# A two-layer kernel on one core: where the shared expert's last products, sums and first additions stand between layer 0 and layer 1

## The chip, the core and the metric

The kernel runs on one NeuronCore of a Trainium2 chip. The time is the device time of one execution in microseconds (us). The profile comes from one further execution that the hardware profiler recorded. The engines are named as in the profile: PE is TensorE's matmul, PEld its weight load, DVE is VectorE, ACT is ScalarE, POOL is GpSimd, SP is SyncE, which here only issues transfers. A name such as L908 is a line of the kernel before.

## What is computed

Two transformer layers over 2048 tokens of 128 channels, all in float32. Both begin with a normalisation and an attention. Layer 0 goes on with a mixture of 16 experts of which each token uses one, plus a shared expert that every token passes. Layer 1 goes on with a gated channel mix. Cut to the part around the change:

```python
h = layernorm(x) * (1 + cb) + sb                      # layer 0, second half
logits = h @ router_w.T
top_vals, top_idx = top_k(logits, 1)                  # one expert of 16 for each token
routed = sigmoid(top_vals) * h                        # sent to that expert alone
expert_sum = (up * silu(gate)) @ down_proj            # gate, up = routed @ gate_up_proj
shared = silu(h @ shared_gate_w.T) * (h @ shared_up_w.T) @ shared_down_w.T
x = x + gb * (shared + expert_sum)
h = layernorm(x) * (1 + ca) + sa                      # layer 1, first half
k, v, q = h @ Wk, h @ Wv, h @ Wq                      # causal attention follows
```

## The kernel before

The tokens lie in 16 tiles of 128, and four tiles make a block of 512 (`TB` = 4, `NB` = 4). `x` stays in SBUF as tiles of 128 tokens by 128 channels; each half of a layer adds its result to it.

**Layer 0's end.** The attention runs over blocks and groups of heads. While its last block is being attended, blocks 0 to 2 are already normalised and routed. What is left when the attention's last weights are done is written out by hand as a list of small steps in `last0`, and `tc.manual_schedule` makes PE, DVE and ACT carry them out in just this order. The list does two things side by side. It finishes block 3: `divide`, `turn_back`, `project`, then the normalisation (`moment`, `norm`, `turn`), the router (`choose`), each token's place in its expert's list (`place`), and `send`, whose four indirect DMAs from POOL (L799) write the rows to DRAM by expert. Between these steps it computes the shared expert for block 0 in four quarters `k`: `up(k, 0)` and `up(k, 1)` are the gate's and the up projection's matmuls (L888), `silu(k)` is ACT's activation (L893), `times(k)` is DVE's product (L897), and `down(k)` adds the quarter's down projection to a sum in PSUM (L901). Quarters 0 and 1 use two PSUM tiles, and quarters 2 and 3 use them again. `add` puts the sum into `x` (L908).

One step of the list is `tiles` (L846 to L870), a chain of small DVE operations. From the count of tokens of each expert it works out how many tiles of 128 each expert needs, and leaves in `nth_i` the start row and the expert of each of the 31 tiles. SP loads the start rows into registers (L1008) and then reads each tile from DRAM (`xs`, L1018). PE loads the expert numbers into registers in the same way, later.

**The experts.** After layer 0 the shared expert has twelve quarters left, four for each of the blocks 1 to 3. `shared_step` takes one: two halves of matmuls (`shared_up`, L991), then the down projection of the quarter before (`shared_down`, L979), then ACT's Silu (L965) and DVE's product (L971; both in `shared_act`). At a block's last quarter `shared_down` also adds the block's sum to `x` (L984). Three quarters run while the tiles are fetched. Then `xs` is transposed by PE (L1031), the experts run over quads of four tiles, and three more quarters are strewn among them. The experts' results go to DRAM (`y_rows`, L1063). Sixteen indirect DMAs on POOL gather them by token (`yx`, L1096) while PE works on the last six quarters.

**Layer 1's beginning**, still in the written order. After the last Silu, ACT changes its table to Sqrt (`table`, L1160). `add(0)` adds the gathered rows of block 0 to `x` (L1110); `moments` takes mean and variance (L204, L205), the root (L217) and its reciprocal (L219); `norm` makes the normalised rows (L252), and `turn` transposes them on PE (L259) and lets ACT write `h2` (L260). The same follows for block 1. `keys` and `queries` are matmuls (L295) whose results ACT scales into a temporary (L296) and DVE writes (L297); `values` is L1127. Then ACT changes to the Exp table, the written order ends, and layer 1's attention starts (L411 is its first scores).

The list at the end of layer 0 closes so:

```python
lambda: up(2, 0), lambda: silu(2), lambda: send(made[0]), lambda: ends_at(made[1]),
lambda: up(2, 1), lambda: up(3, 0), lambda: silu(3), lambda: up(3, 1), tiles,
lambda: times(2), lambda: down(2), lambda: times(3), lambda: down(3), add]
```

## Time and profile before

| | us |
|---|---|
| median of 3 runs (lowest to highest) | 1252.55 (1251.54 to 1255.32) |
| the profiled execution's own time | 1254.59 |
| its span, from the first to the last instruction | 1252.9 |
| PE busy in it | 1156.8 (92%) |
| DVE busy | 943.9 (75%) |
| ACT busy | 780.3 (62%) |
| POOL busy | 94.4 (8%) |

The mean clock granted to TensorE is 0.944 of full speed. Start times are counted from the span's start. In the timelines a line gives the start, the duration, the engine, the line of the kernel, the operation, what it writes and reads, how many such instructions follow each other, and in brackets how long the engine was idle before it and what ended that. In the table of stretches a line gives the stretch, its length, the busy time of PE, PEld, DVE, ACT and POOL with their instructions in brackets, the granted clock, the DMA engines' share and GB/s. The chain of waits is the chain of work that ended last, followed back from the last instruction.

### The profile page before, as it was taken

What the parts mean: (1) busy time and instruction counts of PE and PEld (TensorE: products, weight loads), DVE (VectorE), ACT (ScalarE), POOL (GpSimd) and SP (SyncE); (2) the same over time, 40 slices, a digit from 0 to 9 for tenths busy, and PEclk for the clock granted to TensorE, in tenths of its full rate; (3) what the DMA queues carried; (4) which work ended last, traced back from release to release, by engine and by line L of the source; (5) the groups of instructions that cost most, each with busy time, mean ns of one, the idle gap of its engine ahead of it and who ended that gap; (6) DMA issues with size and microseconds to landing.
All of it is one profiled execution on the core that took longest, in us unless ns stands there. A gap on an engine that the chain in (4) does not pass through costs nothing.

```text
span 1252.9 us, 22356 instructions
## 1 busy us (share of the span) xinstructions
PE 1156.8 (92%) x9230; PEld 523.6 (42%) x9230; DVE 943.9 (75%) x1462; ACT 780.3 (62%) x853; POOL 94.4 (8%) x157
## 2 busy tenths in 40 slices
PE   4579999999999999999999999979978989999985
PEld 2233434444343443443344333447734444444432
DVE  3888898889889889889889983343378788897134
ACT  6107777777777777777777778743333455656763
POOL 2002000000000000000000000320232011110113
PEclk9658999999999999999999999999977899999987
DMA  4841010203220213110000000032210101000001
GB/s 122 112 52 35 2 52 1 70 27 77 69 69 12 59 36 98 38 52 2 1 3 2 1 2 2 20 122 76 66 45 7 35 1 35 1 1 2 2 1 34
DMA packets 63094, 45.22 MB, mean 36 GB/s; under 512 B 6608, under 2 KB 56912, under 8 KB 62480
## 3 DMA queue, kind: packets, MB, share of 16 engines
q1 hardware_dynamic: 60224, 40.37, 13.2%
q0 software_dynamic: 1024, 2.10, 0.6%
q10 hardware_dynamic: 1744, 1.32, 0.6%
q8 instruction: 73, 1.20, 0.4%
q14 instruction: 29, 0.24, 0.1%
HBM read 9.88 MB, written 21.95 MB: 25 GB/s over the span
## 4 chain that ended last, share of the span: by engine, by line
PE 82%; DVE 10%; ACT 4%; issue 1%; DMA 1%; POOL 1%; ACTq 0%; POOLq 0%; DVEq 0%
PE a0bank L502 24%; PE a0p L476 17%; PE a0p L411 13%; PE a1bank L502 5%; PE a1p L476 4%; DVE a0mx L415 3%; DVE a1mx L415 2%; PE a1p L411 2%; PE a1p L482 2%; PE sg L991 2%; DVE a1masked L420 2%; ACT a0e L486 1%; PE gu L1043 1%; PE a0bank L533 1%; PE sum L979 1%
## 5 line engine op out<-in xcount | busy, mean ns | idle before, releaser
L415 DVE TENSOR_REDUCE a0mx<-a0p 128x2 f32<-128x1024 f32 x512 | 624.0, 1225 | 75.9 <-PE a0p L411 66.5
L486 ACT ACTIVATE a0e<-a0p 128x1024 f32<-128x1024 f32 x512 | 522.6, 1025 | 171.9 <-PE a0p L476 146.2
L502 PE MATMUL a0bank<-a0e,vA 128*32 128x256 f32 x4096 | 333.4, 392 | 0.8 <-ACT a0e L486 0.8
L411 PE MATMUL a0p<-kS,a0qS 64*128 64x512 f32 x1024 | 248.1, 480 | 24.7 <-DVE a0mx L415 13.0
L476 PE MATMUL a0p<-a0qS,kS 64*128 64x512 f32 x1024 | 260.6, 498 | 0.0
L486 ACT ACTIVATE a1e<-a1p 128x1024 f32<-128x1024 f32 (+3 forms) x160 | 143.1, 897 | 97.6 <-PE a1p L482 92.3
L476 PEld LDWEIGHTS a0p<-a0qS,kS 64*128 64x128 f32 x1024 | 97.3, 184 | 204.5 <-issue 128.7
L411 PEld LDWEIGHTS a0p<-kS,a0qS 64*128 64x128 f32 x1024 | 100.3, 192 | 109.4 <-ACT a0e L486 56.8
L502 PEld LDWEIGHTS a0bank<-a0e,vA 128*32 128x32 f32 x4096 | 86.4, 108 | 137.9 <-issue 124.4
L415 DVE TENSOR_REDUCE a1mx<-a1p 128x2 f32<-128x1024 f32 x96 | 115.8, 1222 | 17.8 <-PE a1p L411 17.2
L502 PE MATMUL a1bank<-a1e,vA 128*32 128x256 f32 (+1 forms) x1152 | 96.9, 385 | 0.4 <-POOL a1e L489 0.4
L476 PE MATMUL a1p<-a1qS,kS 64*128 64x512 f32 (+3 forms) x320 | 76.3, 463 | 4.9 <-DVE a1mx L415 3.7
L411 PE MATMUL a1p<-kS,a1qS 64*128 64x512 f32 (+3 forms) x320 | 67.7, 422 | 11.2 <-DVE a1mx L420 4.4
L420 DVE CUSTOM_DVE_ANT_0 a1masked<-a1p,later 128x128 f32<-128x128 f32 (+3 forms) x128 | 62.6, 489 | 13.4 <-PE a1p L411 7.5
L799 POOL DMA_INDIRECT sent<-hs,row_i x16 | 15.9, 995 | 712.6 <-DVE ln11xn L252 689.5
L482 PE MATMUL a1p<-a1mT,a1ones 64*128 64x512 f32 (+3 forms) x320 | 62.2, 375 | 0.0
L476 PEld LDWEIGHTS a1p<-a1qS,kS 64*128 64x128 f32 x320 | 31.5, 189 | 61.6 <-issue 32.3
L411 PEld LDWEIGHTS a1p<-kS,a1qS 64*128 64x128 f32 x320 | 32.2, 195 | 39.5 <-DVE a1mx L420 11.5
L489 POOL TENSOR_SCALAR_AFFINE_SELECT a1e<-a1e 128x256 f32<-128x256 f32 x64 | 26.0, 406 | 255.4 <-ACT a1e L486 255.4
L502 PEld LDWEIGHTS a1bank<-a1e,vA 128*32 128x32 f32 x1152 | 25.8, 109 | 42.8 <-issue 32.6
L445 ACT CAST a0mT<-a0bank 8x512 fp32r<-8x512 f32 x16 | 9.2, 576 | 45.4 <-PE a0bank L444 45.4
L482 PEld LDWEIGHTS a1p<-a1mT,a1ones 64*128 64x128 f32 x320 | 32.2, 193 | 2.3 <-issue 1.7
(340 smaller groups left out, 718.2 us busy)
## 6 DMA issues: line engine op xcount, KB each, us to landing
sent<-blank SPq DMA_DIRECT2D x68, 256.0 KB
kS<-a0qS SPq DMA_DIRECT2D x28, 128.0 KB
wgu_sb<-in_gate_up SPq DMA_DIRECT2D x1, 2048.0 KB
a0qS<-a0qh SPq DMA_DIRECT2D x62, 32.0 KB
a0qS<-a0ql SPq DMA_DIRECT2D x62, 32.0 KB
xs<-sent SPq DMA_DIRECT2D x31, 64.0 KB
y_rows<-y SPq DMA_DIRECT2D x7, 256.0 KB
a1qS<-a1qh SPq DMA_DIRECT2D x24, 64.0 KB
```

What stands on the lines that cost most here:

```text
L411: nc.tensor.matmul(ps[:, j, :n], qS[b][r:r + RT, st, i * P:(i + 1) * P], kS(st)[r:r + RT, kb * QB:kb * QB + n], start=True, stop=True)
L415: nc.vector.tensor_reduce(pm[:, i, 2 * pair:2 * pair + 2, kb], ps, AX.X, ALU.max)
L420: nc.vector.tensor_tensor_reduce(masked[:, :n], ps[:, j, :n], later[:, QB - n:], 1.0, LOWEST, ALU.add, ALU.max, pm[:, i, g, kb:kb + 1])
L476: nc.tensor.matmul(ps[:, j, q0:], kS(st)[r:r + RT, kt * P:(kt + 1) * P], qS[b][r:r + RT, st, q0:], start=True, stop=fused)
L482: nc.tensor.matmul(ps[:, j, q0:], ones[r:r + RT, g // S, :], shift[u][r:r + RT, q0:], start=False, stop=True)
L486: nc.scalar.activation(e[:, :, q0:], ps[:, :, q0:], AF.Exp, scale=scale)
L489: nc.gpsimd.affine_select(out=e[:, :, q0:q0 + P], in_=e[:, :, q0:q0 + P], compare_op=ALU.is_ge, fill=0.0, base=0, pattern=[[0, 2], [1, P]] ...
L502: nc.tensor.matmul(av[g * W:(g + 1) * W, c0:c1], vA(kt, grp * HG + g), held[kt, g // 2][:, g % 2, c0:c1], start=(kt == 0 and c0 == 0), sto ...
L533: nc.tensor.transpose(ps[:, i * P:(i + 1) * P], o[:, i * P:(i + 1) * P], ident)
L799: nc.gpsimd.indirect_dma_start(out=sent[t], in_=hs[:, i, :], in_offset=None, out_offset=bass.IndirectOffsetOnAxis(ap=row_i.bitcast(U32)[:, ...
L979: nc.tensor.matmul(sums[b][:, i * P:(i + 1) * P], act[:, i * P:(i + 1) * P], wsd[:, k, :], start=(k == 0 and i == 0), stop=(k == NS - 1), ...
L991: nc.tensor.matmul(ps[:, j, :], w[:, k * P:(k + 1) * P], hT[:, b * QB:(b + 1) * QB], start=True, stop=True)
```

## The change

At the end of layer 0 the second halves of quarters 2 and 3 come ahead of their Silu, and `tiles` takes a function `between`, which it calls twice in the middle of its chain: there `times(2)` and `down(2)`, then `times(3)` and `down(3)` are issued. They used to stand behind the whole of `tiles`.

At the beginning of layer 1 one more quarter of the shared expert leaves the loop. Its matmuls are followed at once by those of the last quarter, and two sums are issued only after them. `add(0)` becomes four additions of one tile each, and each stands before that tile's statistics. The last quarter's product (`last_times`) moves to where the root is computed, and its sum, with the addition of block 3's result, moves from between the queries to right behind `add(1)`, ahead of block 1's statistics. `statistics` takes the number of parts as an argument; with its default it issues what it did.

```diff
+    def moments(b, name, root=False, between=lambda: None, before=lambda i: None):
-        mv, steps = statistics(b, name)
-        for step in steps:
+        mv, steps = statistics(b, name, TB)
+        for i, step in enumerate(steps):
+            before(i)
             step()
...
-    def tiles():
+    def tiles(between):
...
         nc.vector.tensor_tensor(over, ntile.unsqueeze(1).to_broadcast([P, NE, NE]), earlier,
                                 ALU.mult)
+        between(2)
         nc.vector.tensor_reduce(base, over, AX.X, ALU.add)
...
         nc.vector.memset(nth, 0.0)
+        between(3)
         nc.vector.tensor_reduce(nth[:, 1, :SLOTS], passed[:, :, 1:], AX.X, ALU.add)
...
-                lambda: up(2, 0), lambda: silu(2), lambda: send(made[0]), lambda: ends_at(made[1]),
-                lambda: up(2, 1), lambda: up(3, 0), lambda: silu(3), lambda: up(3, 1), tiles,
-                lambda: times(2), lambda: down(2), lambda: times(3), lambda: down(3), add]
+                lambda: up(2, 0), lambda: up(2, 1), lambda: silu(2), lambda: send(made[0]),
+                lambda: ends_at(made[1]), lambda: up(3, 0), lambda: up(3, 1), lambda: silu(3),
+                lambda: tiles(lambda k: (times(k), down(k))), add]
...
-        def add(b):
-            ts = slice(b * TB, (b + 1) * TB)
+        def add(b, part=slice(0, TB)):
+            ts = slice(b * TB + part.start, b * TB + part.stop)
...
-        while len(shared) > 1:
+        while len(shared) > 2:
             shared_step()
+        shared_act(*shared_up())()
         up = shared_up()
-        shared_down()
         last_times = shared_act(*up)
         table(AF.Sqrt)
-        add(0)
-        normed[0] = moments(0, "ln20", True)
+        shared_down()
+        shared_down()
+        normed[0] = moments(0, "ln20", True, last_times, lambda i: add(0, slice(i, i + 1)))
         norm(0)
         turn(0, bank)
-        last_times()
         add(1)
+        shared_down()
         normed[1] = moments(1, "ln21", True, lambda: keys(0, bank)())
...
-        shared_down()
         queries(2, po.tile([P, QB], F32, name="qs2", tag="y"))
```

More of the change, by code (lines that the diff above doesn't have):

```diff
@@ L195, in two_layers, with statistics @@
     lnp = ctx.enter_context(tc.tile_pool(name="lnp", bufs=2))
-    def statistics(b, name):
+    def statistics(b, name, parts=2):
         stats = lnp.tile([P, TB, nc.vector.BN_STATS_DIM], F32, name=name + "stats", tag="stats")
@@ L205, in some @@
                 nc.vector.bn_aggr(mv[:, i, :], stats[:, i, :])
-        return mv, [lambda: some(0, TB // 2), lambda: some(TB // 2, TB)]
-    def moments(b, name, root=False, between=lambda: None):
-        mv, steps = statistics(b, name)
-        for step in steps:
+        return mv, [lambda lo=lo: some(lo, lo + TB // parts) for lo in range(0, TB, TB // parts)]
+    def moments(b, name, root=False, between=lambda: None, before=lambda i: None):
+        mv, steps = statistics(b, name, TB)
+        for i, step in enumerate(steps):
+            before(i)
             step()
```

## The prediction

> **What bounds the kernel now.** I read the page's chain of waits first: PE has 82% of it, DVE 10%. The attention lines (L502, L476, L411, L415) carry most and the change leaves them alone, so I went to the two stretches it edits: layer 0's end (815 to 860 us) and layer 1's beginning (884 to 932 us), by the timeline of each engine. Layer 0's end:

> ```profile
> 836.20 0.42 DVE L852 TENSOR_TENSOR over<-ntile,earlier 128x256 f32<-128x256 f32 x1
> ...
> 840.31 0.18 DVE L870 CAST nth_i<-nth 1x64 int32<-1x64 f32 x1
> 840.41 1.27 DVE L897 TENSOR_TENSOR s0act<-s0act,s0ps 128x512 f32<-128x512 f32 x2
> 841.14 3.78 PE L901 MATMUL s0ps<-wsd_sb,s0act 128*128 128x128 f32 x16 [2.34 <-DVE s0act L897]
> 843.15 15.87 SPq L1018 DMA_DIRECT2D xs<-sent  x31
> 844.96 0.69 DVE L908 TENSOR_TENSOR x<-x,s0ps 128x512 f32<-128x512 f32 x1 [3.28 <-PE s0ps L901]
> 845.70 2.08 PE L991 MATMUL sg<-hT,wsg_sb 128*128 128x512 f32 x2 [0.78 <-DVE x L908]
> ...
> 855.68 1.07 PE L1031 MATMUL xsT_ps<-ident,xs 128*128 128x128 f32 x8 [0.30 <-issue]
> ```

> PE finished its last `up` at 838.79 and stood 2.34 us until the tiles' numbers were done and DVE had made `times(2)`. The first L991 then waited for the `add` (L908). So PE waits for DVE twice. The granted clock comes from the stretches view, which I cut at the clock's own changes:

> ```profile
> 833.65:837.06 3.41, 2.59 (x6) 0.68 (x4) 3.16 (x10) 0.64 (x2) 1.50 (x2) 1.00 0.47 130
> 837.06:840.48 3.42, 1.12 (x2) 0.30 (x2) 3.21 (x10) 0.56 (x1) 2.57 (x3) 1.00 0.12 38
> 840.48:843.89 3.41, 2.75 (x13) 2.75 (x14) 1.20 (x3) 0.00 (x0) 0.00 (x0) 0.50 0.06 19
> 843.89:847.30 3.41, 2.63 (x7) 1.57 (x7) 0.69 (x1) 0.00 (x0) 0.00 (x0) 0.50 0.40 116
> 847.30:850.72 3.42, 3.42 (x5) 1.35 (x4) 0.45 (x1) 0.60 (x1) 0.00 (x0) 0.50 0.47 132
> ```

> Layer 1's beginning:

> ```profile
> 906.60 0.69 DVE L1110 TENSOR_TENSOR x<-x,yx 128x512 f32<-128x512 f32 x1
> ...
> 908.57 1.28 ACT L1160 ACT_TABLE_LOAD   x1
> ...
> 910.91 1.23 PE L259 MATMUL a1bank<-ident,ln20xn 128*128 128x128 f32 x4 [2.08 <-DVE ln20xn L252]
> ...
> 918.28 1.40 PE L979 MATMUL sum<-wsd_sb,acts 128*128 128x128 f32 x8
> ...
> 923.86 0.44 PE L411 MATMUL a1p<-kS,a1qS 64*128 64x128 f32 x4 [1.09 <-DVE a1qS L297]
> ```

> ACT's last Silu ends 908.57, the table load 909.85, block 0's root 910.27; PE stands 2.08 us for the normalised rows. The clock halves from 912.16 to 918.98, and PE then bounds keys, queries and sum until 922.3.

> **Part A: layer 0's end.** No instruction is added or removed, none moved issues a DMA. GpSimd's four sends (835.25 to 840.24) keep their place; only `nth_i` shifts for SP.
> - PE: `up(2,0)` starts 833.15 as now. Now `up(k,1)` waits for `silu(k)` (L888 idle 0.69 and 0.75); both gates now come first. Four halves at 0.86 (pace of L991 at full clock): 833.15 + 3.44 = 836.6, tail to 836.75.
> - `silu(2)` waits for both halves: 835.05 to 835.65. `silu(3)`: 836.8 to 837.4.
> - DVE: `times(2)` after L852: 836.66 to 837.34, so `down(2)` 837.4 to 838.5 (1.13, as the L901 at 827.48). `times(3)` after L854, L857, L861: 838.6 to 839.3; `down(3)` 839.3 to 840.4.
> - The chain of the tiles' numbers carries both: `nth_i` ends 840.49 + 1.27 = 841.76. The `add` follows (sums long ready): 841.7 to 842.37. First L991 at 842.42 instead of 845.70: **3.28 us**.
> - Clock, on the traced grid: 837.06 to 840.48 now has some 2.2 of 3.42 us busy, kept. 840.48 to 843.89 has 1.4 to 1.5, lost. 843.89 to 847.30 is full (three steps of L991 in a row), returned. One halved stretch instead of three.
> - PE until the gathered rows: six `up` halves pairs and two sums, 3 x 1.72 + 2 x 0.89 = 6.94 us at full clock. 842.42 to 843.89 does 1.47, the halved stretch 1.71, the remaining 3.76 end 851.07. PE's own load of `nth_i` (L1008, 2.32 us, from 853.3 now, just after the second step's `times`) starts about 849.1, ends 851.4: xsT at 851.4 instead of 855.68, **-4.3 us**.
> - What hides the later `nth_i`: SP's load of it (L1008, 2.16 us, straight after the cast) ends 843.95 instead of 842.7, first xs read at 844.42, one each 0.51 us. The eighth goes out at 848.0; to landing I have no row for it, the nearest (sent 2.2, yx 2.5, at most 3.1) give 850.2 to 851.1. Needed about 851.9. Cover is 0.8 us; gone, each us late is a us lost.
> - `times` beside GpSimd's sends: ln21xn beside the gathers took 436 ns against 344, so 0 to 0.2 us; I take 0.
> Bounds: the clock falls at 840.48 too or stays down, -3.3; it never falls, PE would end 849.4 and the load 849.6, -6.1 (xs would then bind). I take -4.3.

> **Part B: layer 1's beginning** (times of the trace before the shift).
> - The last two gates run together and the sums go behind: last L991 ends 907.04 instead of 907.93, Silu 907.68, table 908.97, ready 909.18.
> - DVE: the 0.69 add becomes four of 128x128 (L538: 0.29). A tile is add, L204, L205 with 0.1 us of gaps and overlap: 0.71, x4 from 906.60: 909.5 against 909.01. Root 909.55 to 909.83. `times(3,3)` runs beside it, 909.44 to 910.12; reciprocal 910.04 against 910.29. Gain 0.25.
> - The gathers reach block 0 at 903.90 and block 1 at 908.80 (landings in the trace), before use.
> - PE: four transposes, then the sum that stood at 918.28, in front of keys. It fills the wait for hT (0.87 idle now) at full clock; halved it takes 1.8, ending 913.9.
> - New wait: block 3's add (L984, 0.69) is now ahead of block 1's statistics and waits for that sum: it ends 913.64 (full) or 914.6 (half), statistics (1.70) 915.3 or 916.3 against 914.68. Behind them ACT's root and the scaled keys, so kS starts 916.3 or 917.25 against 915.84. That is a loss at this point.
> - After kS: qS0, norm(1), qS1, qS2, vA, qS3: DVE needs 4.4 to 5.0 and no longer carries L984 and `times`. Last qS ends 921.4 at full clock. Halved with the clock back near 918, PE's queries end 921.1 and the last qS 922.6. Now it ends 923.80. So -2.4 or -1.2; should PE stay halved throughout, keys to last query take it to some 925.5, minus a return that comes at latest one full stretch on: bound +0.5.
> With the shift of part A the grid cuts the 2 us gap in two (0.97 and 1.02 idle), so full clock is rather likelier: I take **-1.8**.

> Sum: -4.3 - 1.8 = -6.1. The profiled execution took 1254.59 us (span 1252.9 and 1.7 around it): 1248.5. It lies 2.0 above the median of 1252.55, and the other runs may have their grid elsewhere; the same difference on the median gives **1246.5**.

> [...]

> **Rivals.**
> 1. The clock eats it: it halves at 840.48 too and stays down at layer 1. Then only the earlier start is left: -3.3 and 0, 1249.2. For: the grid isn't tied to the program, and the gaps left (0.9 and 2.0 us) fill one stretch on many phases. Against: the traced phase. 0.20.
> 2. Neither gap halves it: -6.1 - 2.4 = -8.5, 1244.0. For: 0.59 busy kept it. Against: 2.0 us of wait for the `add` remains. 0.20.
> 3. Slower: the shift moves layer 1's opening on the clock grid. From 925 to 985 us the mean clock is 0.69, so 22.8 of 60 us are at full. If all ran halved and half of it lies on the chain, it costs 11.4: +5.3, 1257.9. It decides from 6.1 us of chain work lost to half clock. Against: from 985 on the clock is 1.00, and the same 3.41 us rule would have to fail almost every stretch. 0.05.
> 4. It doesn't do what it says: the first L991 is not set free by the `add`, or xs lands late. Part A falls to -2 to -3, total near 1248. Against: L991 starts 0.05 after L908 ends. 0.05.

> **Numbers.** Forecast 0.50, its own range 1244.5 to 1248.6. About 0.3% (3.8 us) is what a measurement can tell from no change: faster means under 1248.8. Forecast, rival 2 and part of 4 lie there: 0.72; rival 1 and the edges 0.23; slower 0.05. Range 1243.0 (rival 2 with 1 us of spread, the runs shown span 3.8) to 1250.6 (part A at -3.3 with part B at +0.5, and 0.9 of spread).

> **What would show it.** L901 in two groups of 8, among the tiles' lines; first L991 3.3 us earlier against L888; one halved stretch there, not three; xsT 4.3 us earlier; SP's first xs read some 1.3 us later; at layer 1 the L979 directly behind L259 and the last L297 1.2 to 2.4 us earlier against L1031. It is wrong if PE waits for xs, if kS is late and nothing makes it up, or if halved stretches after 925 us grow.

## The result and the profile after

| | before | after |
|---|---|---|
| median (lowest to highest), six runs each | 1253.07 us (1251.54 to 1255.32) | 1247.64 us (1246.41 to 1249.66) |
| profiled execution | 1254.59 us | 1248.58 us |
| its span | 1252.9 us | 1246.9 us |
| mean granted clock | 0.944 | 0.947 |

The ratio is 0.9956, with a 95% interval of 0.9942 to 0.997: faster by 5.4 us, and by 6.0 us between the two profiled executions. The forecast was 6.1 us and 1246.5 us. The changed kernel is three lines longer behind the change, so L888 is now L891, L901 is L904, L908 is L911, L979 is L982, L991 is L994, L1031 is L1034 and L297 is L298.

Layer 0's end in the timeline of the changed kernel, PE first, then DVE and SP:

```profile
837.67 1.16 PE L904 MATMUL s0ps<-wsd_sb,s0act 128*128 128x128 f32 x8 [0.46 <-DVE s0act L900]
839.31 1.16 PE L904 MATMUL s0ps<-wsd_sb,s0act 128*128 128x128 f32 x8 [0.49 <-DVE s0act L900]
842.38 1.10 PE L994 MATMUL sg<-hT,wsg_sb 128*128 128x512 f32 x2 [1.91 <-DVE x L911]
849.85 1.07 PE L1034 MATMUL xsT_ps<-ident,xs 128*128 128x128 f32 x8 [0.21 <-issue]
...
836.93 0.68 DVE L900 TENSOR_TENSOR s0act<-s0act,s0ps 128x512 f32<-128x512 f32 x1
838.64 0.61 DVE L900 TENSOR_TENSOR s0act<-s0act,s0ps 128x512 f32<-128x512 f32 x1
841.46 0.18 DVE L873 CAST nth_i<-nth 1x64 int32<-1x64 f32 x1
841.56 0.67 DVE L911 TENSOR_TENSOR x<-x,s0ps 128x512 f32<-128x512 f32 x1
```

The sum that was one block of sixteen matmuls and 3.78 us at half clock is now two groups of eight among the tiles' numbers, 1.16 us each. PE's wait is at the `add`: 1.91 us. The first shared matmul behind it starts at 842.38; the forecast said 842.42. The transposes of the fetched rows start at 849.85 where 851.4 was forecast and 855.68 stood before. The clock says why, in the stretches of the changed kernel on the clock's grid (length, then busy time of PE, PEld, DVE, ACT and POOL, then clock, DMA share and GB/s):

```profile
840.90:844.31 3.41, 1.93 (x5) 1.00 (x6) 1.26 (x4) 0.00 (x0) 0.00 (x0) 1.00 0.06 19
844.31:847.72 3.41, 3.41 (x15) 1.81 (x14) 1.38 (x2) 1.20 (x2) 0.00 (x0) 1.00 0.33 96
```

No stretch is at half clock; there were three before and the forecast left one. The forecast had the clock lost after the wait for the `add`, with 1.4 to 1.5 us of work in the stretch (there 840.48 to 843.89). The grid lay 0.42 us later than before, so that the stretch held 1.93 us (57%), and the clock stayed.

Layer 1's beginning in the timeline of the changed kernel:

```profile
906.13 1.92 PE L982 MATMUL sum<-wsd_sb,acts 128*128 128x128 f32 x8
908.08 0.69 DVE L987 TENSOR_TENSOR x<-x,sum 128x512 f32<-128x512 f32 x1 [1.68 <-PE sum L982]
...
911.32 0.75 DVE L298 SCALAR_TENSOR_TENSOR kS<-a1bank,low,a1tmp 128x512 fp32r<-128x512 f32 x1 [0.94 <-ACT a1tmp L297]
912.30 1.28 POOL L316 TENSOR_TENSOR x<-x,a1bgrows 128x512 f32<-128x512 f32 x1
912.71 1.74 DVE L253 TENSOR_SCALAR ln21xn<-x,ln21mv,ln21y 128x128 f32<-128x128 f32 x4
...
915.92 0.75 DVE L298 SCALAR_TENSOR_TENSOR a1qS<-a1bank,low,a1tmp 128x512 fp32r<-128x512 f32 x1
915.82 1.00 PE L260 MATMUL a1bank<-ident,ln21xn 128*128 128x128 f32 x4 [1.97 <-DVE a1qS L298]
```

The eight matmuls of the last sum stand directly behind block 0's transposes and take 1.92 us, the price forecast for half clock (1.8); DVE waits 1.68 us for them before block 3's addition.

The whole is summed over four stages: up to the router's first matmul, from there to the first transpose of the fetched rows (`xs`), on to the end of the last scaled query, and the rest. First the kernel before, then the changed one, by stretches with the same columns; the first stage, the same in both, is left out.

```profile
830.09:855.68 25.59, 20.73 (x78) 12.68 (x78) 11.65 (x31) 5.72 (x8) 4.07 (x4) 0.80 0.44 127
855.68:923.80 68.12, 62.48 (x328) 46.13 (x328) 30.55 (x68) 25.66 (x44) 18.00 (x19) 0.95 0.19 55
923.80:1252.88 329.08, 290.96 (x2324) 138.01 (x2324) 222.93 (x541) 173.52 (x210) 40.23 (x74) 0.91 0.05 14
```

```profile
830.47:849.85 19.38, 16.31 (x77) 10.27 (x78) 11.11 (x31) 5.73 (x8) 4.20 (x4) 1.00 0.42 122
849.85:916.67 66.82, 61.16 (x328) 46.17 (x328) 30.93 (x71) 25.54 (x44) 18.56 (x19) 0.97 0.24 69
916.67:1246.88 330.21, 293.76 (x2325) 139.68 (x2324) 222.94 (x542) 173.58 (x210) 40.39 (x74) 0.90 0.05 14
```

Everything up to the router is 0.38 us later (830.47 against 830.09), part A's stage is 6.21 us shorter, part B's 1.30 us shorter, and layer 1's attention 1.13 us longer. That is -6.00 us. The three differences belong to this pair of profiles; the experiments show how much of them lies in where the clock's grid fell. In the first 100 us of the attention the mean clock was 0.81 before and is 0.76 after.

### The profile page after: what moved, and what is told of

It reads as the page before. It is cut to its first block, busy times and chain, and to the rows that moved or that the text cites. A ratio compares the mean times of both kernels' runs of the same rounds, so it can differ in the third digit from the quotient of the medians.

```text
span 1246.9 us, 22357 instructions
## 1 busy us (share of the span) xinstructions
PE 1154.3 (93%) x9230; PEld 523.0 (42%) x9230; DVE 943.5 (76%) x1465; ACT 780.2 (63%) x853; POOL 95.3 (8%) x157
## 4 chain that ended last, share of the span: by engine, by line
PE 81%; DVE 11%; ACT 4%; issue 1%; DMA 1%; POOL 1%; ACTq 0%; POOLq 0%; DVEq 0%
PE a0bank L503 24%; PE a0p L477 17%; PE a0p L412 13%; PE a1bank L503 6%; PE a1p L477 4%; DVE a0mx L416 3%; PE a1p L412 2%; PE a1p L483 2%; DVE a1mx L416 2%; DVE a1masked L421 2%; PE sg L994 2%; ACT a0e L487 1%; PE gu L1046 1%; PE a0bank L534 1%; PE a0bank L445 1%
```

## The experiments

My theory: part A is worth some 4 us and more because it closes PE's 2.34 us wait, and with it saves halved clock; part B shortens layer 1's beginning by little. The rivals: the order alone does it without the clock; the earlier `up` halves do it; part B's gain is eaten by its late addition for block 3, by its gathers, or by the clock of layer 1's attention.

Three chips ran these kernels, and each ratio is against the kernel before on the same chip: 1253.73 us on the first (the first four experiments), 1254.26 us on the second (the next four), 1265.22 us on the third (the last four). The row of after is from the first measurement, against 1253.07 us. The ratios are not quotients of the two medians, and differ from them a little (before_filled: 0.9966 beside 1248.09 / 1253.73 = 0.9955). In the table "to xsT" is the stage from the router to the first transpose of the fetched rows, "halved" the time at half clock in it, "to query" the next stage, "attention" the last, and "halved after" the halved time in its first 100 us, summed over the grid's stretches. Stages are of one profiled execution each.

| kernel | median us | ratio (interval) | to xsT | halved | to query | attention | halved after |
|---|---|---|---|---|---|---|---|
| before | | | 25.59 | 10.2 | 68.12 | 329.08 | 37.5 |
| after | 1247.64 | 0.9956 (0.9942 to 0.997) | 19.38 | 0 | 66.82 | 330.21 | 47.7 |
| a_alone | 1250.73 | 0.998 (0.9964 to 0.9995) | 19.38 | 0 | 68.03 | 328.71 | 37.6 |
| b_alone | 1255.34 | 1.001 (0.9994 to 1.0027) | 22.84 | 3.4 | 66.79 | 333.58 | 54.6 |
| before_filled | 1248.09 | 0.9966 (0.9952 to 0.9981) | 21.40 | 0 | 66.75 | 327.55 | 34.1 |
| late_sum | 1247.74 | 0.9966 (0.9952 to 0.998) | 19.38 | 0 | 66.78 | 329.72 | 44.4 |
| after_again | 1249.60 | 0.996 (0.9947 to 0.9973) | 21.08 | 3.4 | 66.81 | 331.30 | 51.1 |
| ups_first | 1254.10 | 1.0003 (0.9992 to 1.0015) | 25.64 | 10.2 | 68.11 | 329.11 | 37.5 |
| whole_add | 1249.62 | 0.9962 (0.9949 to 0.9975) | 19.39 | 0 | 66.72 | 333.32 | 54.6 |
| late_filled | 1244.01 | 0.9923 (0.9911 to 0.9935) | 19.38 | 0 | 64.17 | 328.61 | 44.4 |
| a_alone_2 | 1262.18 | 0.9981 (0.9966 to 0.9996) | 21.09 | 3.4 | 75.43 | 332.09 | 54.6 |
| b_alone_2 | 1262.60 | 0.9973 (0.9955 to 0.9992) | 21.38 | 0 | 74.72 | 332.94 | 51.2 |
| gap_filled | 1258.30 | 0.9953 (0.9933 to 0.9973) | 21.09 | 3.4 | 74.87 | 326.08 | 27.2 |
| a_filled | 1257.30 | 0.9937 (0.9914 to 0.996) | 19.39 | 0 | 76.45 | 329.93 | 44.4 |

**a_alone** is the kernel before with part A only:

```diff
+        between(2)
...
+        between(3)
...
+                lambda: tiles(lambda k: (times(k), down(k))), add]
```

> Only layer 0's end is changed (products and sums of quarters 2 and 3 among the tiles' numbers); layer 1's beginning is as before. My theory: most of the gain is here, because the changed kernel's profile has its first L991 3.7 us earlier and its xsT 6.2 us earlier against layer 0's router, and no halved clock between. -4.3 us (if the clock still halves once on the median execution) to -6.2 us, so 1247 to 1249 beside 1253. Rival, that layer 1's part brings more than half: -2.5 us or less. In its profile the first matmul of the next block's quarter starts 3.7 us earlier against the router than before.

Measured: -3.0 us on medians, 0.998. That is less than the 4.3 to 6.2 us expected and more than the rival's 2.5; the interval, 0.6 to 4.5 us, does not decide between them. In its profile all of part A is there, 19.38 us to xsT and nothing halved, and part B's stage is as before. The timed runs give less than the profile's 6.2 us; the paragraph on a_alone_2 and b_alone_2 says why that can be.

**b_alone** is the changed kernel with the list and `tiles` of layer 0 put back:

```diff
-                lambda: up(2, 0), lambda: up(2, 1), lambda: silu(2), lambda: send(made[0]),
...
+                lambda: up(2, 0), lambda: silu(2), lambda: send(made[0]), lambda: ends_at(made[1]),
```

> Only layer 1's beginning is changed; layer 0's end is as before. My theory: -0.5 to -1.3 us, because block 1's statistics now wait for block 3's sum and most of the earlier start is given back; within noise of the kernel before. Rival, the prediction's own part B: -1.8 us. Other rival, a loss: the new wait outweighs the gain, +0.5 us. The profile counts more than the time here: the last L297 ahead of layer 1's first scores against xsT.

Measured: 1.001, no change that can be told; the prediction's own -1.8 us lies outside this interval. The stage to the last query is 1.33 us shorter (66.79 against 68.12), as in the changed kernel, and the attention behind it 4.5 us longer.

**before_filled** keeps the order of before, and only puts three matmuls, whose result nobody reads, on PE behind the last `up`:

```diff
+        def fill(n):
+            for _ in range(n):
+                nc.tensor.matmul(third[:, 1, :], wsg[:, :P], h1[:, HOFF:HOFF + QB], start=True,
+                                 stop=True)
...
+                lambda: up(2, 1), lambda: up(3, 0), lambda: silu(3), lambda: up(3, 1), tiles, lambda: fill(3),
```

> The kernel before, with three more matmuls of 128x512 (0.86 us each) on PE behind the last up projection, into the half of a PSUM tile that nobody reads any more; they add no result. They fill the 2.34 us in which PE waits for DVE's product, and leave the order of all else. Clock theory: the halved stretches at 840 to 851 us go, the two sums take 1.9 us instead of 3.8 and the next blocks' matmuls run at full clock: -4 to -5 us without any reordering. Order theory, that only the earlier start of PE counts: 0. The 0.8 us wait for the first addition stays in both.

PE in its timeline:

```profile
836.36 2.74 PE L916 MATMUL s0ps<-hT,wsg_sb 128*128 128x512 f32 x6
838.93 1.98 PE L901 MATMUL s0ps<-wsd_sb,s0act 128*128 128x128 f32 x16
841.69 1.13 PE L996 MATMUL sg<-hT,wsg_sb 128*128 128x512 f32 x2 [0.78 <-DVE x L908]
```

The three fillers (L916, six passes) stand where PE waited 2.34 us. Nothing is reordered, and the same sixteen matmuls take 1.98 us instead of 3.78: they run at full clock (1.00 in the mean of the stage, 0.80 before). The stage to xsT is 4.2 us shorter, the kernel 5.6 us faster on medians (ratio 0.9966). So most of what part A takes from this place in its pair of profiles can be had by work without any use. The clock is the larger part of it there, the order the smaller: 21.40 us against the 19.38 us of the new order.

The next stage of this profile bears on part B. Layer 1's beginning stands there as in the kernel before, and yet it takes 66.75 us, as little as with part B. It lost the clock for one stretch, where the kernel before lost it for two (912.16 to 918.98):

```profile
906.11:909.52 3.41, 2.99 (x4) 1.44 (x5) 2.08 (x10) 1.35 (x3) 2.77 (x3) 0.50 0.19 58
909.52:912.93 3.41, 3.41 (x19) 2.21 (x18) 2.87 (x7) 1.68 (x3) 2.56 (x4) 1.00 0.13 38
```

On the first two chips the old order took 68.03 to 68.12 us with two halved stretches (three profiles) and 66.75 us with one (this profile); the new order took 66.72 to 66.82 us with one whole halved stretch in all five profiles without fillers. So the 1.3 us of part B's stage is what one halved stretch less gives in the old order too. Whether it is the new order that saves the stretch, or the draw of the grid, these profiles don't show.

**late_sum** is the changed kernel with block 3's addition (the 0.69 us that waits for the sum) taken out of `shared_down` and issued behind the last queries:

```diff
-            if k == NS - 1:
+            if k == NS - 1 and b < NB - 1:
+                add_sum(b)
...
+        add_sum(NB - 1)
```

> The changed kernel, with the addition of block 3's sum to x taken from ahead of block 1's statistics and put behind the last query on DVE; the sum's matmuls stay ahead of the keys. My theory: the statistics wait 1.68 us for PE there and 0.6 us for the addition, ACT's second root and the scaled keys hang on them, so keys and queries end 0.7 to 1.5 us earlier against xsT; -0.7 to -1.5 us against the changed kernel. Rival, that DVE is the bound after the keys and the addition only moves to its end: 0.

Measured: 0.9966 against 0.9956 and 0.996 of the changed kernel, no difference, and 66.78 us in the stage against 66.82. The expected 0.7 to 1.5 us did not come. Its timeline shows where they went:

```profile
908.98 0.75 DVE L298 SCALAR_TENSOR_TENSOR kS<-a1bank,low,a1tmp 128x512 fp32r<-128x512 f32 x1 [2.06 <-ACT a1tmp L297]
910.51 2.69 DVE L253 TENSOR_SCALAR ln21xn<-x,ln21mv,ln21y 128x128 f32<-128x128 f32 x4
911.05 1.28 POOL L316 TENSOR_TENSOR x<-x,a1bgrows 128x512 f32<-128x512 f32 x1
```

The scaled keys do come earlier: 60.34 us behind xsT (908.98 and 848.64 here) against 61.47 us in the changed kernel (911.32 and 849.85 there). But the next operation, block 1's normalised rows (L253), takes 2.69 us for four instructions. The first of them took 1.92 us, the others 0.34 us. It ended at 912.43, 0.10 us after POOL's addition L316 ended (912.33). In the changed kernel the first took 0.97 us and ended at 913.68, POOL's at 913.58; in the kernel before, 0.74 us, 918.95 and 918.85. Counted from xsT, POOL's addition ends at 63.69 us here and at 63.73 in the changed kernel, so what was won ahead of it was gone when L253's first instruction ended. In nine of the fourteen profiles the first of these instructions overlapped POOL's addition, took 0.59 to 1.92 us and ended some 0.1 us behind it. In the other five the two did not overlap: it took 0.34 us in the four of the third chip, like its companions, and 0.55 us in late_filled, where POOL's addition came after it. In two of the nine (late_sum and after_again) VectorE's instruction had even begun first by the profile, by 0.54 and 0.28 us. That VectorE is held here until GpSimd has finished is read from these times, not from an experiment that removes POOL's addition; that one was not made. What would hold it, no run here shows.

**after_again** is the changed kernel once more, on the chip of the next three.

> The changed kernel once more, so that it can be set beside the parts on the same chip. Single executions of one kernel lie up to 8 us apart (the clock's grid of 3.41 us falls differently on each), so the median of more runs counts: 1247 to 1249, 5 to 6 us under the kernel before. If the parts do not add up (layer 0's end alone gave 0.998, layer 1's beginning alone 1.001), either this comes out near 1250 (the parts add, the first result was lucky) or it stays near 1247.5 (they help each other: layer 0's part moves layer 1's beginning on the grid).

Measured: 0.996 (4.7 us on medians), near the first 0.9956. Its profiled execution lost the clock for one stretch:

```profile
839.48:842.90 3.42, 1.51 (x6) 0.76 (x5) 1.93 (x5) 0.00 (x0) 0.55 (x1) 1.00 0.07 20
842.90:846.31 3.41, 3.41 (x5) 1.33 (x4) 0.69 (x1) 0.60 (x1) 0.00 (x0) 0.50 0.22 64
```

It is the same program: here a stretch begins 9.72 us behind the router (839.48 and 829.76) instead of 10.43 (840.90 and 830.47), and the grid cuts the wait for the `add` so that this stretch holds 1.51 us of work (44%), and the next is halved. It costs 1.70 us (21.08 against 19.38). This is the very stretch that the forecast had: 1.4 to 1.5 us, one halved.

**ups_first** is the kernel before with only the `up` halves put ahead of their Silu:

```diff
+                lambda: up(2, 0), lambda: up(2, 1), lambda: silu(2), lambda: send(made[0]),
+                lambda: ends_at(made[1]), lambda: up(3, 0), lambda: up(3, 1), lambda: silu(3), tiles,
```

> The kernel before with one piece of the change: the second halves of quarters 2 and 3 come ahead of their Silu; products and sums stay behind the tiles' numbers. My theory: PE is done earlier (836.7 instead of 838.8) and then waits longer for DVE's product, 4.4 us instead of 2.3; the first L991 starts as before. 0 in start, and the longer gap can only halve the clock sooner: 0 to +1 us. Rival, that the wait of the second halves for the Silu was itself on the path: -1.5 us.

Measured: 1.0003, and every stage as before. PE runs its halves sooner and then waits 4.32 us instead of 2.34 for `times(2)`. The `up` halves give nothing until the products stand inside the tiles' chain.

**whole_add** undoes the additions by tile:

```diff
-        normed[0] = moments(0, "ln20", True, last_times, lambda i: add(0, slice(i, i + 1)))
+        add(0)
+        normed[0] = moments(0, "ln20", True, last_times)
```

> The changed kernel with block 0's rows added in one 128x512 addition again instead of four, all else kept. The statistics of block 0 then end 0.5 us earlier on DVE (four adds with their gaps take 1.2 us, one takes 0.69), but ACT's table is ready only after the last Silu, so the root gains what the table leaves: about -0.3 us at the root, within noise in the time. Rival, that the gathered rows land late and the whole add has to wait for the fourth tile: +0.5 us or more at block 0's first statistics.

Measured: 0.9962 against 0.996, and 66.72 us against 66.81. The additions by tile give and cost nothing that can be told; if part B gives anything, it comes from the rest of it.

**late_filled** adds to late_sum two matmuls of no use at each of three places where PE waited: behind the two early sums of layer 0 before the `add`, behind the two held-back sums before block 0's transposes, and behind the last queries.

```diff
+                lambda: tiles(lambda k: (times(k), down(k))), lambda: fill(2), add]
...
+        fill(bank(), 2)
...
+        fill(q[0], 2)
+        add_sum(NB - 1)
```

> The changed kernel with the addition of block 3's sum put behind the last query, and matmuls of 128x512 that add no result in PE's three gaps: two ahead of the first L991, two behind the two sums held back, two behind the last query (0.86 us each). Clock theory: no halved stretch at the experts' start on any execution and none or one at layer 1's beginning instead of two: -1.5 to -3.5 us against the changed kernel with the late addition alone, and the executions lie closer together. Rival, that DVE and ACT bound layer 1's beginning and the fillers stand in PE's way: 0 to +1 us.

Measured: 1244.01 us, 0.9923, the fastest of all: the interval (0.9911 to 0.9935) lies under that of the changed kernel. Against late_sum's 0.9966 it is more than the 1.5 to 3.5 us expected, but that one ran on another chip. The stage to the last query takes 64.17 us at a clock of 1.00, 2.6 us less than late_sum's 66.78. The normalised rows of block 1 don't overlap POOL's addition here:

```profile
910.44 1.12 DVE L253 TENSOR_SCALAR ln21xn<-x,ln21mv,ln21y 128x128 f32<-128x128 f32 x4
912.20 2.51 POOL L316 TENSOR_TENSOR x<-x,a1bgrows 128x512 f32<-128x512 f32 x2
```

They come 60.62 us behind xsT (849.82 here) instead of late_sum's 61.87, while POOL's addition starts at 62.38 instead of 62.41: it starts after them, and the four take 1.12 us. Which of the three places gives how much isn't told apart by this run alone; of the first, the halved stretch that after_again shows is the most that it can save by the profiles taken, 1.70 us.

The last four ran on the third chip, where the stage to the last query takes 7 to 8 us more than in the same kernels on the others. ACT stands still there ahead of block 0's transposed rows, for a reason that the trace doesn't name (it says "remote", and PE at the 5.81 us): 10.42 us in b_alone_2 and 10.38 in gap_filled; in the two without part B in two pieces, 4.96 and 7.02 us in a_alone_2, 5.81 and 6.38 in a_filled. The second piece in a_alone_2:

```profile
915.00 0.78 ACT L260 ACTIVATE hT<-a1bank,mod 128x512 f32<-128x512 f32 x1 [7.02 <-remote]
```

These are compared only with the kernel before on that chip.

**a_alone_2 and b_alone_2** repeat the two halves of the change.

> Layer 0's end alone, once more. In the profiles so far its cover from the router to the first transpose of the fetched rows is 19.4 us against 22.8 to 25.6 before, and nothing behind it is slower than before. Theory that layer 1's part gives nothing net: -4 to -6 us here, as much as the whole change (the first set of runs, 0.998, was at the low edge). Rival, that both parts are needed: again -2 to -3 us.

> Layer 1's beginning alone, once more. Theory: 1.3 us are won up to the last query in every profile, and lost behind it, since PE now waits about 2 us for DVE there, which halves the clock: of the 100 us that follow, 44 to 55 us are halved in the profiles with this part and 34 to 38 in those without. Net 0 to +3 us. Rival, that the two are unrelated and this was the draw of the grid: -1.3 us.

Measured: part A alone 0.9981, as the first time, which is nearer to the 2 to 3 us of the rival than to the 4 to 6 us of the theory (the interval is 0.5 to 4.3 us); part B alone 0.9973 (0.9955 to 0.9992), a gain where 0 to +3 us was expected and 1.001 had been measured. Those two intervals don't even overlap, so part B's worth in time is not settled. Part A alone (0.998 and 0.9981) lies above the three measurements of both parts (0.9956, 0.996 and 0.9962), with intervals that overlap at the edge: that part A is the whole of the gain isn't shown either. The profiles of b_alone and b_alone_2 show what else moves: with the old order at layer 0's end, the time halved there was 3.4 and 0 us, where before and ups_first show 10.2. The old order drew 10.2 us twice, 3.4 and 0 in four profiles; the new one drew 0 four times and 3.4 three times in seven (with and without part B, those with fillers at layer 0's end left out). That the grid's position decides the draw is read from pairs such as after and after_again, not from an experiment. The mean of the stage is 23.86 us in four profiles of the old order and 20.11 us in seven of the new, so part A is worth some 3.75 us by this estimate, not the 6.2 of one pair of profiles. The draws are few, but it stands within the 0.6 to 4.5 us that a_alone's interval allows. At full clock the old order takes 21.4 us (before_filled 21.40, b_alone_2 21.38) and the new one 19.38. By these means the order is worth 2.0 us and the clock 1.7, about as much each; in the first pair of profiles the clock was the larger part.

**gap_filled** is the changed kernel with two useless matmuls behind the last queries, where part B leaves PE waiting 1.97 us before the first scores:

```diff
+        fill(q[0], 2)
```

> The changed kernel with two matmuls of 128x512 that add no result behind the last query, so that PE is not idle for 2 us ahead of layer 1's first scores; nothing else. Theory that this gap is what layer 1's part pays with: the halved stretch around the last query goes or is shorter, the halved time in the next 100 us falls to 34 to 40 us, -1.5 to -3 us against the changed kernel. Rival, that the halved time there is decided later (attention's own gaps): 0.

Measured: 0.9953 on that chip, and the least halved time in the attention of all, 27.2 us in its first 100, with the shortest attention, 326.08 us. The ratio doesn't tell it from the changed kernel's 0.9956 and 0.996 on the other chips; the 1.5 to 3 us expected against that kernel are neither shown nor excluded. This is what the theory expects by which PE's new wait starts the halved stretches. But a_alone_2, which has no part B, has 54.6 us of it, and the kernel before loses the clock at this place too: PE is busy for 1.36 of the 3.41 us from 922.40, and the stretch behind them is halved. One run for, these against: that the gap is the cause isn't shown.

**a_filled** is part A with fillers at the three places and without part B:

```diff
+                lambda: tiles(lambda k: (times(k), down(k))), lambda: fill(2), add]
...
+        fill(bank(), 2)
...
+        fill(q[0], 1)
```

> Layer 0's end changed, layer 1's beginning as before, with matmuls that add no result in PE's gaps: two ahead of the first L991, two ahead of layer 1's first transposes, one behind the last query. Beside the kernel with both parts and fillers (0.9923) it tells what layer 1's new order is worth when the clock is kept up. Theory: PE bounds keys and queries here only at half clock, DVE at full; the new order then brings its 1.3 us: this comes out 1 to 1.5 us above that kernel, near 0.993 to 0.994. Rival, that the order is worth nothing beside the clock: 0.992.

Measured: 0.9937 (0.9914 to 0.996), on another chip than late_filled's 0.9923 (0.9911 to 0.9935). The intervals overlap: whether part B still adds something once PE is kept busy stays open.

## Why the prediction was right, point by point

**The sum.** Forecast -6.1, measured -6.0 between profiled executions and -5.4 on medians. But its terms were -4.3, -1.8 and 0, and came out at -6.2, -1.3 and +1.1 (and +0.38 of drift before the change begins). In after_again they were -4.5, -1.3 and +2.2. Three errors made up for each other in part, so that the number came out so near is partly luck.

**Part A, the start: right mechanism, too small.** The first shared matmul came 3.70 us earlier, measured from the router, where 3.28 was forecast. The term that was off is the price of the two products inside the tiles' chain, put at 1.27 us, their whole duration. `nth_i` moved by 0.77 us only: 11.17 us from the router to the end of the cast, against 10.40. The reading of the timeline, which no run tests: the chain's own operations wait for each other, and the products use some of that time. In the kernel before, a step starts some 0.04 us after the step that it needs has ended. The second L900 runs from 838.64 to 839.25 while the next step of the chain already starts at 839.19.

**Part A, the clock: the step holds as a mechanism, and the count was one of two.** One halved stretch was forecast; the profile had none, after_again had one. Rival 2 had given -6.1 for none, and 6.21 was measured. before_filled shows that it is the clock: the old order at full clock takes 4.2 us off the stage. The border at 0.55 of a stretch does not hold. At layer 0's end the fourteen profiles lost the clock after stretches with up to 1.51 us busy and kept it from 1.76 us (late_sum) upwards. Elsewhere it was lost after more: in the kernel before after 2.19 us (973.60 to 977.01) and after 2.71 us. First late_sum, then before:

```profile
839.51:842.92 3.41, 1.76 (x4) 0.87 (x5) 1.44 (x4) 0.00 (x0) 0.02 (x1) 1.00 0.06 19
842.92:846.34 3.42, 3.42 (x15) 1.95 (x14) 1.38 (x2) 1.19 (x2) 0.00 (x0) 1.00 0.31 86
...
929.22:932.64 3.42, 2.71 (x17) 1.71 (x16) 2.52 (x11) 0.59 (x1) 0.00 (x0) 1.00 0.18 43
932.64:936.05 3.41, 1.32 (x6) 0.58 (x4) 3.05 (x10) 0.00 (x0) 0.00 (x0) 0.50 0.41 107
```

The return is no simpler. At layer 0's end the clock was back after a fully busy stretch at half clock (3.42 of 3.42 us from 847.30 in the kernel before). In the changed kernel the stretch from 970.61 was as full (3.41 of 3.42 us), and the next, to 977.44, was halved too; so the return "at latest one full stretch on", which the forecast's bound of +0.5 took, does not hold either. PE's busy share alone does not decide, and what else does, these runs don't show.

**Part A, the cover: held.** The rows arrived in time; SP read the first at 844.24 and PE began its transposes at 849.85, when its own load of the expert numbers (2.32 us from 847.5) had ended. Rival 4 falls. What wasn't taken at a cost, `times` beside GpSimd's sends, cost nothing (0.68 and 0.61 us, against 1.27 us for both before).

**Part B: the number of one of the two ends, the cause not shown.** I took -1.8 from -2.4 at full clock and -1.2 at half. The sum ran halved (1.92 us from 906.13, in the stretch from 905.75 to 909.16 at 0.50) and the stage came out 1.3 us shorter, so the choice of the clock was wrong. That it fits the -1.2 does not show the order at work: before_filled had the same stage as short without part B, with one halved stretch instead of two. The first terms are there as forecast: the last gate matmul ends 51.36 us after xsT instead of 52.26, the sum fills PE's wait, block 3's addition is late and kS with it (10.10 us after the last gate instead of 7.90). What was missing is L253's first instruction, which ended 0.10 us behind POOL's addition (913.68 and 913.58). The forecast had met it and not seen it: its 436 ns for ln21xn "beside the gathers" is the mean of one instruction of 0.74 us, which overlapped POOL's addition, and three of 0.34. By this reading moving the addition away (late_sum) gave nothing, though the forecast saw it as the loss of part B.

**Behind the last query: missed.** I had nothing there but rival 3 (slower, from 6.1 us of halved work). In part it happened: 1.1 and 2.2 us were given back, with 47.7 and 51.1 us of halved time in the first 100 us, against 37.5. Over all kernels the attention takes some 0.25 us more for each such halved us. That is a straight line through the fourteen profiles and no experiment. Whether part B or the grid's draw decides it stays open, by a_alone_2 and gap_filled.

## What to carry to other kernels

A wait of PE can cost more than itself: behind the 2.34 us here stood three stretches of 3.41 us at half clock in the kernel before. Price it by the halved stretches behind it, for several positions of the grid, and judge by the mean over runs, not by one profile pair. A short independent operation put into a chain of dependent ones can cost less than its duration: two products of 0.68 and 0.61 us moved the chain's end by 0.77 us. Where an engine has nothing to do but wait, a few useless matmuls are a cheap test of whether the clock is what the wait costs, and here they also made the kernel faster (0.9966 for three in before_filled).

## What the runs showed of the hardware

Not expected were VectorE's instruction that ended some 0.1 us behind GpSimd's addition wherever the two overlapped (the first of L253, 0.59 to 1.92 us in nine profiles, where its three companions took 0.34), and ACT's waits of 4.96 to 10.42 us on one chip, whose releaser the trace gives as "remote" for all but one. The same program kept or lost the clock at layer 0's end between one execution and the next, with 57% (after) and 44% (after_again) of a stretch busy; elsewhere it was lost after 79% (before, 929.22 to 932.64).
